# Output tiles of three pairs instead of four, in the same 48 KB, for the last 204 pairs of a pairwise bilinear kernel

## The chip, the cores and the metric

The kernel runs on one core of one Trainium2 chip. The metric is the device time of one execution in microseconds (us). A core has TensorE (PE: matmuls; PEld: its weight loads), VectorE (DVE), ScalarE (ACT), GpSimd (POOL), SyncE (SP), and 16 DMA engines that carry everything between the chip's memories. SyncE, ScalarE and GpSimd issue the DMAs, each on a queue of its own.

## The reference

There are 32 fields; each has, for 1024 rows of a batch, a vector of 128 numbers. For each of the 496 pairs of fields i < j there is a 128 x 128 matrix W. The result of a pair is the vector of field i times the pair's matrix, and that times the vector of field j, number by number:

```python
v_i = inputs[:, I_IDX, :]
v_j = inputs[:, J_IDX, :]
transformed = jnp.einsum('bpd,ped->bpe', v_i, W)
return transformed * v_j
```

All is in 32-bit floats. The output has 496 x 128 x 1024 of them, 260 MB; the inputs together have 49 MB.

## The kernel before, in words

**Tiles.** Fields lie on the chip as tiles of 128 partitions (the 128 numbers) by 1024 (the batch). The pairs are taken in the order of falling i and rising j; `q` is a pair's place in that order, 0 to 495. A pair's result is 128 x 1024, 4 KB a partition, 512 KB in all. It is made in two halves of 512, and `u = 2q + h` counts halves.

**One half.** The first 15 pairs are multiplied as plain 32-bit floats (L233). For all others the operands are split: ScalarE makes a high part (`wh` L142, `xh` L160), GpSimd the rest (`wl`, `wd` L144 to L146, `xl` L161 and L162), VectorE `xd` (L300). A half is then two matmuls (L236), a scaling of the sum in place by ScalarE (L238) and a third matmul that adds to it (L247), three halves later (`LAG`). There are four PSUM tiles `po`, so PE may be four pairs ahead of VectorE at most. VectorE multiplies a whole pair by field j and writes it to an output tile (L257, `ot`); the last two pairs go by halves (L255).

**Stores.** `OG = 4` pairs in succession share an output tile of 16 KB a partition (`out_tile`, L214). When the fourth is written, ScalarE issues one DMA for the tile (L284), 2 MB in rows of 16 KB. The issue stands in ScalarE's queue behind the scaling of the half that is five later (`SLAG` and `LAG`), and waits there for VectorE. The first group, and the last four pairs, are stored by single pairs or halves.

**Which tiles.** Three output tiles, s0 to s2, are there all the time (48 KB a partition). Four more, g0 to g3, are the places in which four fields each are loaded later on; until 20 pairs before that load (`until`, L211) they serve as output tiles too. `out_tile` takes the one that was used longest ago. From some pair on only s0, s1, s2 and g0 go round, and g0 is given up at pair 293, so that group 73 (pairs 292 to 295) is the first with three tiles alone. A tile is written again when its store has landed.

**Loads.** Matrices come eight pairs at a time (`load_w`, 512 KB), through SyncE, or as 448 KB through GpSimd and 64 KB through SyncE (`load_apart`, L106); a load is issued when the buffer before it has been split up. The fields of g0 are loaded from pair 313 on (`load_group`, L112), one in six pairs. `move_on` (L102) issues tiny loads through GpSimd.

**Order.** The order is written out by hand: the loop at L266 emits for each `u` the first part of that half, the second part of the half three before, stores that are due (L283), splits that are due (L285), loads and `xd`. Each engine takes its instructions in that order and waits on semaphores.

Of the kernel before, what the change touches and what calls it, by code (L numbers as in the profile page):

```python
# [7 lines left out]
F32 = mybir.dt.float32  # L8
F32R = mybir.dt.float32r
ALU = mybir.AluOpType  # L10

P = 128
NF = 32
NQ = NF * (NF - 1) // 2
BT = 1024
HB = 512
WC = 2
WL = 8
OG = 4
# [15 lines left out]
ROWS = 8 * NE  # L35
WAPART = tuple(range(12, 62, 2))
BACK = 3
XAT = (313, 219, 141, 52)
OWAIT = 20
XSTEP = 6  # L40
SLAG = 2
# [3 lines left out]
def _pairs():  # L45

    return [(i, j) for i in range(NF - 2, -1, -1) for j in range(i + 1, NF)]


@with_exitstack  # L50
def kernel(
# [21 lines left out]

    nc = tc.nc
    pairs = _pairs()
    nchunk = NQ // WC

    xpool = ctx.enter_context(tc.tile_pool(name="x", bufs=1))
# [3 lines left out]
    opool = ctx.enter_context(tc.tile_pool(name="o", bufs=1))  # L82
    ppool = ctx.enter_context(tc.tile_pool(name="ps", bufs=1, space=bass.MemoryType.PSUM))

    x_sb = {}
# [41 lines left out]
    scaled, taken, halved = {}, {}, {}  # L127

    def apart(inst, other, reason="the halves of a pair lie in two banks"):

        if other is not None:
            tc.declare_no_dep(inst.ins, other.ins, reason=reason)
# [75 lines left out]
    ngroup = NF // XG // 2  # L208
    group_at = {q + XSTEP * (XG - 1 - m): (k, m) for k, q in enumerate(XAT) for m in range(XG)}
    assert all(q + 5 < first_q[XG * k + m + 2] for q, (k, m) in group_at.items())  # L210
    until = {f"g{k}": q - OWAIT for k, q in enumerate(XAT)}  # L211
    used = {t: n - 9 for n, t in enumerate(("s0", "s1", "s2", *sorted(until, reverse=True)))}

    def out_tile(g):  # L214
        t = min((t for t in used if (g + 1) * OG <= until.get(t, NQ + OG)), key=used.get)
        used[t] = g
        pool = xpool if t in until else opool
        return pool.tile([P, OG, BT], F32, tag=t, name=f"ot_{g}")

    ctx.enter_context(tc.manual_schedule())  # L220
    po, ots, stores = {}, {}, []
# [19 lines left out]
    def second(u):  # L241
        q, h = divmod(u, 2)
        i, j = pairs[q]
        r = slice(q % WC * P, (q % WC + 1) * P)
        s = slice(h * HB, (h + 1) * HB)
        if q >= nq0:
            m = nc.tensor.matmul(  # L247
                po[q][:, s], w_s[q // WC][2][:, r], x_s[i][2][:, s], start=False, stop=True, skip_group_check=True
            )
            apart(m, scaled[u ^ 1])  # L250
        g, k = divmod(q, OG)
        if k == 0 and h == 0:
            ots[g] = out_tile(g)
        if q >= NQ - 2:
            nc.vector.tensor_tensor(ots[g][:, k, s], po[q][:, s], x_sb[j][:, s], ALU.mult)  # L255
        elif h == 1:
            taken[q] = nc.vector.tensor_tensor(ots[g][:, k, :], po.pop(q), x_sb[j], ALU.mult)  # L257
        if q >= NQ - 2:
            stores.append((u + SLAG, out[g, :, k, s], ots[g][:, k, s]))
        elif g == 0 or q >= NQ - OG:  # L260
            if h == 1:
                stores.append((u + SLAG, out[g, :, k], ots[g][:, k]))
        elif k == OG - 1 and h == 1:
            stores.append((u + SLAG, out[g], ots[g]))

    for u in range(2 * NQ + LAG + SLAG):  # L266
        q = u // 2
        if u < 2 * NQ:
            i, j = pairs[q]
# [11 lines left out]
        if LAG <= u < 2 * NQ + LAG:  # L281
            second(u - LAG)
# [7 lines left out]
        if ring[WB:] and ring[0] in spent:  # L290
# [6 lines left out]
            if c in WAPART:  # L297
                back.append(q + BACK)
        while later and later[0][0] <= u:
# [32 lines left out]
```

## Time and profile before

| | |
|---|---|
| median of 5 runs | 747.72 us (745.5 to 749.06) |
| the profiled execution: its own time | 748.25 us |
| its span, from first to last instruction | 746.5 us |
| busy: PE, DVE, ACT, POOL | 706.3, 637.9, 635.2, 596.6 us |
| moved by DMA | 310.02 MB, 415 GB/s over the span |
| output stores of 2048 KB | 122, 12.1 us from issue to landing in the median |

Busy time is the time in which an engine worked; one that waits is not busy. A DMA share near 1 over a stretch means that all 16 DMA engines had packets in work in it; the sum can come out at 1.01, since one packet's record can overlap the next by a little. A granted clock (PEclk) of 1.00 is TensorE at full speed. A line number, such as L257, is that of the listing above.

### The profile page before, as it was taken

Reading aid. Unit: us, or ns where it says so; the run is one execution under the profiler, and the core shown is the slowest. Engines: PE = TensorE matmul, PEld = TensorE weight load, DVE = VectorE, ACT = ScalarE, POOL = GpSimd, SP = SyncE. Lnnn points to the kernel's source line nnn. Section 1 sums busy time; section 2 is a strip of 40 time slices with the busy share of each in tenths; the row PEclk is TensorE's granted clock in tenths of the full one; section 3 lists DMA queues with packets and bytes.
Section 4 is the critical chain, followed back from the end, with each engine's and each line's share of the span. In section 5 each row is a group of like instructions: output and inputs, shape, how many; then the busy total and the mean of one; then the engine's idle time right before and its main releaser. Section 6 shows DMA issues by size and latency. Waiting matters only on the chain.

```text
span 746.5 us, 10290 instructions
## 1 busy us (share of the span) xinstructions
PE 706.3 (95%) x2946; PEld 550.1 (74%) x2946; DVE 637.9 (85%) x550; ACT 635.2 (85%) x1256; POOL 596.6 (80%) x882
## 2 busy tenths in 40 slices
PE   7999999999999999899899979998999999999994
PEld 3477777777778887677688858877877878777783
DVE  3898999999999998898799868878998989888885
ACT  1198989999999999798899968988988989888893
POOL 1789999999999999878779867977787888796660
PEclk9999999999999999999999989999999999999998
DMA  9999999999999999999999998999999999999998
GB/s 347 425 428 424 418 406 430 423 417 430 419 415 421 427 423 422 427 428 419 424 428 422 428 426 343 424 423 423 425 424 419 420 421 419 418 405 398 423 405 343
DMA packets 34664, 310.02 MB, mean 415 GB/s; under 512 B 5296, under 2 KB 5424, under 8 KB 18992
## 3 DMA queue, kind: packets, MB, share of 16 engines
q10 hardware_dynamic: 19584, 261.10, 83.1%
q1 hardware_dynamic: 10592, 36.77, 12.4%
q0 software_dynamic: 4432, 11.48, 4.1%
q8 instruction: 24, 0.39, 0.2%
q14 instruction: 32, 0.26, 0.1%
HBM read 49.29 MB, written 260.05 MB: 414 GB/s over the span
## 4 chain that ended last, share of the span: by engine, by line
PE 60%; DMA 23%; DVE 9%; POOL 3%; issue 2%; ACT 1%; DVEq 0%; ACTq 0%; POOLq 0%
PE po L236 38%; DMA out_dram<-ot 22%; PE po L247 19%; DVE ot L257 6%; PE po L233 4%; DVE xd L300 2%; POOL wd L146 1%; POOL wl L144 1%; POOL xl L161 1%; DMA x<-in_xt_dram 1%; ACT po L238 1%; POOL xl L162 0%; POOL wd L145 0%; DVE ot L255 0%; ACT wh L142 0%
## 5 line engine op out<-in xcount | busy, mean ns | idle before, releaser
L238 ACT ACTIVATE po<-po 128x512 f32<-128x512 f32 x962 | 553.3, 584 | 78.1 <-PE po L236 62.5
L257 DVE TENSOR_TENSOR ot<-po,x 128x1024 f32<-128x1024 f32 x358 | 430.5, 1221 | 74.6 <-DMA out_dram<-ot 25.4
L236 PE MATMUL po<-xh,wh 128*128 128x512 f32 x962 | 382.3, 397 | 22.2 <-DVE ot L257 21.4
L247 PE MATMUL po<-xd,wd 128*128 128x512 f32 x962 | 376.0, 391 | 4.8 <-DVE xd L300 2.4
L236 PE MATMUL po<-xl,wl 128*128 128x512 f32 x962 | 376.9, 392 | 1.3 <-POOL wl L144 0.9
L236 PEld LDWEIGHTS po<-xh,wh 128*128 128x128 f32 x962 | 181.0, 188 | 80.8 <-DVE ot L257 43.9
L144 POOL TENSOR_TENSOR wl<-w,wh 128x256 fp32r<-128x256 f32 x241 | 185.5, 770 | 68.5 <-ACT wh L142 62.3
L247 PEld LDWEIGHTS po<-xd,wd 128*128 128x128 f32 x962 | 181.0, 188 | 45.0 <-DVE ot L255 3.2
L236 PEld LDWEIGHTS po<-xl,wl 128*128 128x128 f32 x962 | 181.2, 188 | 41.0 <-POOL wl L144 4.0
L146 POOL TENSOR_TENSOR wd<-wl,wd 128x256 fp32r<-128x256 f32 x241 | 181.4, 753 | 20.1
L257 DVE TENSOR_TENSOR ot<-po,x_g 128x1024 f32<-128x1024 f32 x136 | 163.9, 1223 | 25.5 <-DMA out_dram<-ot 12.9
L145 POOL TENSOR_SCALAR wd<-wh 128x256 fp32r<-128x256 f32 x241 | 103.2, 428 | 20.5
L142 ACT ACTIVATE wh<-w 128x256 fp32r<-128x256 f32 x241 | 98.6, 410 | 8.3 <-DVE ot L257 5.8
L300 DVE TENSOR_TENSOR xd<-xh,xl 128x512 fp32r<-128x512 f32 x52 | 49.1, 944 | 0.0
L161 POOL TENSOR_TENSOR xl<-x_g,xh 128x512 fp32r<-128x512 f32 x32 | 41.7, 1302 | 3.2 <-ACT xh L160 3.0
L161 POOL TENSOR_TENSOR xl<-x,xh 128x512 fp32r<-128x512 f32 x20 | 25.8, 1292 | 15.8 <-ACT xh L160 15.5
L162 POOL TENSOR_SCALAR xl<-xl 128x512 fp32r<-128x512 f32 x52 | 34.4, 662 | 4.6
L233 PE MATMUL po<-x,w 128*128 128x512 f32 x60 | 30.5, 669 | 4.0 <-DMA x<-in_xt_dram 4.0
L233 PEld LDWEIGHTS po<-x,w 128*128 128x128 f32 x60 | 12.4, 212 | 21.3 <-issue 15.5
L160 ACT ACTIVATE xh<-x 128x512 fp32r<-128x512 f32 x20 | 12.3, 623 | 11.5 <-DMA x<-in_xt_dram 11.3
L160 ACT ACTIVATE xh<-x_g 128x512 fp32r<-128x512 f32 x32 | 20.0, 624 | 0.0
L104 POOL DMA_DIRECT2D mark<-in_xt_dram x26 | 16.6, 638 | 0.0
(7 smaller groups left out, 20.0 us busy)
## 6 DMA issues: line engine op xcount, KB each, us to landing
out_dram<-ot ACTq DMA_DIRECT2D x122, 2048.0 KB, 12.1
w<-in_wt_dram SPq DMA_DIRECT2D x36, 512.0 KB, 10.9
w<-in_wt_dram POOLq DMA_DIRECT2D x25, 448.0 KB, 11.9
x_g<-in_xt_dram SPq DMA_DIRECT2D x16, 512.0 KB, 16.5
x<-in_xt_dram SPq DMA_DIRECT2D x14, 512.0 KB, 9.6
out_dram<-ot ACTq DMA_DIRECT2D x6, 512.0 KB, 8.3
w<-in_wt_dram SPq DMA_DIRECT2D x26, 64.0 KB, 6.3
x<-in_xt_dram ACTq DMA_DIRECT2D x4, 256.0 KB, 5.9
```

Of the source, the lines that this page charges most:

```text
L142: halved[c] = nc.scalar.mul(h, raw, 1.0 - 2.0**-13)
L144: nc.gpsimd.tensor_tensor(l, raw, h.bitcast(F32), ALU.subtract)
L145: nc.gpsimd.tensor_scalar(d, h.bitcast(F32), EPS, 1.0, ALU.mult, ALU.mult)
L146: nc.gpsimd.tensor_tensor(d, l.bitcast(F32), d.bitcast(F32), ALU.subtract)
L161: nc.gpsimd.tensor_tensor(l, x_sb[f][:, s], h.bitcast(F32), ALU.subtract)
L162: nc.gpsimd.tensor_scalar(l, l.bitcast(F32), 1.0 / EPS, 1.0, ALU.mult, ALU.mult)
L233: nc.tensor.matmul(po[q][:, s], w_raw[q // WL][:, q % WL, :], x_sb[i][:, s], start=True, stop=True)
L236: m = nc.tensor.matmul(po[q][:, s], w_s[c][t][:, r], x_s[i][t][:, s], start=t == 0, stop=t == 1)
L238: scaled[u] = nc.scalar.mul(po[q][:, s], po[q][:, s], 1.0 + EPS)
L247: m = nc.tensor.matmul(po[q][:, s], w_s[q // WC][2][:, r], x_s[i][2][:, s], start=False, stop=True, skip_group_check=True)
L257: taken[q] = nc.vector.tensor_tensor(ots[g][:, k, :], po.pop(q), x_sb[j], ALU.mult)
L300: nc.vector.tensor_tensor(*later.pop(0)[1:], ALU.subtract)
```

## The change

The first 73 groups (pairs 0 to 291) stay as they are, four pairs each. From pair 292 on there are 68 groups of three pairs. The three tiles s0 to s2 become one tile `slots` of 12 places of one pair each (the same 48 KB a partition); a group of four on s0, s1 or s2 takes places 0 to 3, 4 to 7 or 8 to 11, and groups of three take places 0 to 2, 3 to 5, 6 to 8 and 9 to 11 in turn. Which store a product has to wait for is then found by places. `written` and `apart` declare that two products of VectorE on the same place need no wait on each other. The output in memory becomes one run of 496 pairs, in which a group of n pairs lies as 128 rows of n x 4 KB; the host puts it in order. The last group, pairs 493 to 495, is stored by a single pair and by halves, as the last four pairs were.

```diff
+FOURS = 73
+NS = 12
...
+def _groups():
+
+    return [(q, OG) for q in range(0, OG * FOURS, OG)] + [(q, OG - 1) for q in range(OG * FOURS, NQ, OG - 1)]
...
+    groups = _groups()
+    group_of = {q + k: (g, k) for g, (q, n) in enumerate(groups) for k in range(n)}
...
+    slots = opool.tile([P, NS, BT], F32, tag="slots", name="slots")
+    written = {}
+
     def out_tile(g):
-        t = min((t for t in used if (g + 1) * OG <= until.get(t, NQ + OG)), key=used.get)
-        used[t] = g
-        pool = xpool if t in until else opool
-        return pool.tile([P, OG, BT], F32, tag=t, name=f"ot_{g}")
+        q, n = groups[g]
+        if n < OG:
+            a = (g - FOURS) * n % NS
+        else:
+            t = min((t for t in used if q + n <= until.get(t, NQ)), key=used.get)
+            used[t] = g
+            if t in until:
+                return xpool.tile([P, OG, BT], F32, tag=t, name=f"ot_{g}"), None
+            a = OG * int(t[1:])
+        return slots[:, a : a + n, :], a
+
+    def rows(g):
+        q, n = groups[g]
+        return out[q : q + n].rearrange("q a -> (q a)").rearrange("(p k m) -> p k m", p=P, k=n)
+
+    def write(g, k, s, p, f):
+        ot, a = ots[g]
+        i = nc.vector.tensor_tensor(ot[:, k, s], p, f, ALU.mult)
+        if a is not None:
+            for h in (0, 1):
+                if s.start < (h + 1) * HB and s.stop > h * HB:
+                    apart(i, written.get((a + k, h)), "one engine writes both, in order")
+                    written[a + k, h] = i
+        return i
...
-        g, k = divmod(q, OG)
+        g, k = group_of[q]
...
-        elif g == 0 or q >= NQ - OG:
+        elif g in (0, len(groups) - 1):
             if h == 1:
-                stores.append((u + SLAG, out[g, :, k], ots[g][:, k]))
-        elif k == OG - 1 and h == 1:
-            stores.append((u + SLAG, out[g], ots[g]))
+                stores.append((u + SLAG, rows(g)[:, k], ot[:, k]))
+        elif k == n - 1 and h == 1:
+            stores.append((u + SLAG, rows(g), ot))
```

More of the change, by code (lines that the diff above doesn't have):

```diff
@@ L254, in second @@
         if q >= NQ - 2:
-            nc.vector.tensor_tensor(ots[g][:, k, s], po[q][:, s], x_sb[j][:, s], ALU.mult)
+            write(g, k, s, po[q][:, s], x_sb[j][:, s])
         elif h == 1:
-            taken[q] = nc.vector.tensor_tensor(ots[g][:, k, :], po.pop(q), x_sb[j], ALU.mult)
+            taken[q] = write(g, k, slice(0, BT), po.pop(q), x_sb[j])
+        ot = ots[g][0]
+        n = groups[g][1]
         if q >= NQ - 2:
-            stores.append((u + SLAG, out[g, :, k, s], ots[g][:, k, s]))
-        elif g == 0 or q >= NQ - OG:
+            stores.append((u + SLAG, rows(g)[:, k, s], ot[:, k, s]))
+        elif g in (0, len(groups) - 1):
             if h == 1:
-                stores.append((u + SLAG, out[g, :, k], ots[g][:, k]))
-        elif k == OG - 1 and h == 1:
-            stores.append((u + SLAG, out[g], ots[g]))
+                stores.append((u + SLAG, rows(g)[:, k], ot[:, k]))
+        elif k == n - 1 and h == 1:
+            stores.append((u + SLAG, rows(g), ot))
     for u in range(2 * NQ + LAG + SLAG):
@@ L323 @@
         args.append(nc.dram_tensor(f"in_{name}_dram", a.shape, mybir.dt.from_np(a.dtype), kind="ExternalInput").ap())
-    args.append(nc.dram_tensor("out_0_dram", (-(-NQ // OG), P, OG, BT), F32, kind="ExternalOutput").ap())
+    args.append(nc.dram_tensor("out_0_dram", (NQ, P * BT), F32, kind="ExternalOutput").ap())
     with tile.TileContext(nc) as tc:
@@ L329 @@
     y = _np.empty((BT, NQ, P), _np.float32)
-    y[:, perm, :] = got.transpose(3, 0, 2, 1).reshape(BT, -1, P)[:, :NQ]
+    for q, n in _groups():
+        y[:, perm[q : q + n], :] = got[q : q + n].reshape(P, n, BT).transpose(2, 1, 0)
     return y
```

## The prediction

> **What bounds the kernel now.** I read the page's slices and its DMA queues first, then the chain, then busy time by stretches, then VectorE in order of time around pair 292. From the page:
>
> ```profile
> DMA  9999999999999999999999998999999999999998
> GB/s 347 425 428 424 418 406 430 423 417 430 419 415 421 427 423 422 427 428 419 424 428 422 428 426 343 424 423 423 425 424 419 420 421 419 418 405 398 423 405 343
> ...
> q10 hardware_dynamic: 19584, 261.10, 83.1%
> ...
> PE 60%; DMA 23%; DVE 9%; POOL 3%; issue 2%; ACT 1%; DVEq 0%; ACTq 0%; POOLq 0%
> ```
>
> The 16 DMA engines are busy in nearly every slice; one slice (the 25th, 448 to 466 us) moves 343 GB/s instead of some 424. q10, the output stores, is 83% of their time. The chain names PE for 60%, but a chain walks through whatever was last at each step; PE's pace and the DMA's are close. One pair of halves is six matmuls; VectorE's undisturbed products stand 1.36 us apart (716.57, 717.93, 719.29 us), so PE alone would bring out 512 KB in 1.36 us, and the DMA at 424 GB/s takes 1.24 us for that plus the loads. So I ask by stretch who is full:
>
> ```profile
> core 0: us, PE busy (x) PEld busy (x) DVE busy (x) ACT busy (x) POOL busy (x), PEclk, DMA share, GB/s
> 20.00:430.00 410.00, 398.04 (x1677) 311.34 (x1676) 369.21 (x321) 362.60 (x722) 358.89 (x520) 1.00 1.01 423
> ...
> 438.00:444.00 6.00, 1.35 (x6) 0.77 (x5) 0.35 (x1) 2.00 (x5) 4.43 (x8) 0.88 1.02 433
> 444.00:448.00 4.00, 3.07 (x7) 2.51 (x8) 3.83 (x4) 1.05 (x2) 0.00 (x0) 0.50 0.99 426
> 448.00:449.50 1.50, 1.50 (x5) 1.14 (x4) 0.33 (x1) 0.69 (x2) 0.00 (x0) 0.54 0.59 251
> 449.50:451.25 1.75, 1.75 (x10) 1.40 (x9) 1.42 (x2) 1.39 (x3) 0.40 (x1) 1.00 0.13 56
> 451.25:453.25 2.00, 2.00 (x10) 1.67 (x9) 1.84 (x2) 1.79 (x5) 1.83 (x4) 1.00 0.94 393
> ...
> 470.00:700.00 230.00, 222.05 (x951) 176.28 (x951) 198.01 (x170) 206.22 (x407) 185.28 (x280) 1.00 1.01 419
> ...
> 716.00:735.00 19.00, 18.89 (x84) 15.31 (x82) 17.11 (x15) 17.03 (x33) 9.52 (x16) 1.00 0.94 395
> ...
> 744.00:745.00 1.00, 0.00 (x0) 0.00 (x0) 0.00 (x0) 0.00 (x0) 0.00 (x0) 0.50 0.12 47
> ```
>
> The column before the last is the DMA share. It is 1.01 from 20 to 430 us and from 470 to 700 us: **the DMA engines are full, and VectorE's waits for tiles cost nothing there**. They are idle in two places only. One hole lies at 448 to 451.5 us: 1.5 x 0.41 + 1.75 x 0.87 + 2 x 0.06 = 2.3 us in the mean over 16 engines. The other is the end, 716 to 735 us: 19 x 0.07 (against 1.01) = 1.3 us. But 0.13 is two engines of 16: two were busy all through the hole, and two (0.12) finish last, from 744 to 745. What makes the first hole:
>
> ```profile
> 432.19 5.02 DVE L257 TENSOR_TENSOR ot<-po,x 128x1024 f32<-128x1024 f32 x4 [0.27 <-DMA out_dram<-ot]
> 443.65 2.36 DVE L257 TENSOR_TENSOR ot<-po,x 128x1024 f32<-128x1024 f32 x2 [6.44 <-DMA out_dram<-ot]
> 445.92 0.68 DVE L300 TENSOR_TENSOR xd<-xh,xl 128x512 fp32r<-128x512 f32 x1
> 446.62 1.23 DVE L257 TENSOR_TENSOR ot<-po,x 128x1024 f32<-128x1024 f32 x1
> ```
>
> 443.65 is pair 292. Group 73 is the first that can't have g0 and goes to s0, whose store (group 70) lands at 443.53: 6.44 us of waiting. PE stands still, comes back at clock 0.50, and the next store is issued only at 450.56, when the four products are done.
>
> **The change part by part.**
>
> *The wait at pair 292 stays.* Slots 0 to 2 held pairs 280 to 282 of the same group 70, and one store carries them: in the order of the changed program pair 292 waits for the same semaphore as before. Pairs 296 and 300 also wait for the stores of groups 71 and 72 as before. Nothing is saved up to 447.9 us.
>
> *The first store comes earlier.* After three products (292, 293, 294; the last ends at 446.62 + 1.23 = 447.85) instead of four (450.41). ScalarE issues it after the scaling three pairs on, whose rows stand at 448.75 and 449.86, so at 449.3 instead of 450.56: the hole shrinks by 1.2 us, for the 14 engines that had run dry. For the two that never did, by nothing.
>
> *Packets.* Stores of 292 to 495 go out in rows of 12 KB. The trace's packet records have the median of a packet by size: 84 ns (2 KB), 140 (3.5 KB), 159 (4 KB), 611 (16 KB), 9 for the store's semaphore. From 4 to 16 KB that is 150.7 ns for 4 KB and 8 fixed, and the 3.5 KB row lies on the line, so a size that is no power of two costs nothing of its own; 12 KB: 460.3. An engine carries 8 rows of a store: four pairs 8 x 611 + 9 = 4897, 1224 ns a pair; three pairs 8 x 460.3 + 9 = 3691, 1230.5 a pair. 6.3 ns x 201 pairs (the last three go out singly) = **1.3 us more** on every engine. The late engines pay more: of the stores' packets the slowest twentieth takes 94 ns at 2 KB, 174 at 4 KB, 647 at 16 KB (the last in 715 to 735 us, without loads). That line has 16 ns fixed, and 136 packets more on an engine (67 stores of three, 536 rows, against 50 of four, 400) are 2.2 us. Ends 1.3 and 2.2; I take 1.7.
>
> *Sixteen stores more on ScalarE's queue*, 0.34 us each (row of the issue at 450.56). The next scaling starts 0.11 us after such an issue (450.67), beside it: 16 x 0.1 = 2 us of an engine that idles 20.8 us from 475 on. Nothing, while the DMA is full; if that cover went, 2 us. In the changed order a store also waits for the DMA eight issues earlier on SP's and ScalarE's queues, as before; eight issues are now some 17 pairs (24 us) against landings of 8.9 to 17.2 us, so it has landed. SP's loads have such waits too, and weights behind them; the same margin covers them.
>
> The Trainium skill ("DMA: Bandwidth & Descriptors", "Anatomy of one DMA") gives a DMA 2.0 us and its bytes at 436 GB/s, and its rule of sizes asks for 1 MiB and more a DMA, which 1.5 MB still is. If each store paid the 2.0 alone, 16 more would be an estimated 32 us by that page. Share 1.01 with two stores outstanding says that it lies beside the next store; the sum goes without it.
>
> *A longer lead.* At a boundary three tiles of three (9 pairs) may be outstanding instead of two of four (8), in the same 48 KB. With the engines full this only moves the waits. At the end it counts: PE's last wait for a tile ends at 706.1 us and from there products come at PE's pace to 739.2; one pair of lead is 1.2 us, and smaller stores leave shorter gaps. But at least three engines are busy at every instant of 716 to 735 us, by the packet records. Engines that idle there gain at most 1.3 us; those that end last gain nothing that the trace shows.
>
> *The sum* goes by the engines that end last: +1.7, less what they win from the hole. If the two of 450 us are the two of 745, that is 0; if others, at most their lag of 1.0 us behind the rest. The trace does not name engines: I take -0.4. +1.3 on the profiled execution's 748.25 us is 749.5. It lies 0.5 above the median of the five runs (747.72), so against the median: **749.0 us**.
>
> **Rivals.**
>
> *Holes filled (faster).* If the late engines change places, the hole (1.2, at most 2.3) and the end (1.3) are won, and 1.3 paid: -1.2 to -2.3, 745.4 to 746.5. For it: both idle places are caused by stores of four pairs. Against it: two engines are never idle.
>
> *Packets dearer (slower, the other side of no change).* One mechanism: in every store from pair 292 a 12 KB row costs an engine more than the line says. An engine has 536 such packets, so 1 ns is 0.54 us; the sum passes 0.3% (2.2 us, with -0.4 for the hole) when the rows cost 2.6 us, that is from (2.6 - 1.3) / 0.54 above 460, some 463 ns. If a row were moved as three of 4 KB (3 x 159 = 477), an engine would pay (8 x 477 + 9) / 3 - 1224 = 51 ns a pair, 10.3 us: 758. At the late engines' 16 ns of fixed cost alone it is 2.2 us, 749.9. For it: packets of those engines. Against 477: the 3.5 KB row, and 16 KB packets are recorded whole.
>
> *No lead at all.* A store lands when the last engine is done, and the late two lag by 3 to 4 us at pair 292, by the landings of the 16 engines; the fourth tile would then only wait on them, and the change is the packets alone: 1.3 to 2.2, 749.0 to 749.9. This lies beside the forecast.
>
> **How the numbers follow.** Measurement of this kernel tells some 0.3% (2.2 us) from no change: 745.5 to 750.0. Forecast and "no lead", within 0.3%: 0.55. Packets dearer: 0.30, most of it just beyond 750.0, a sixth of it near 758. Holes filled: 0.15, of which 0.10 below 745.5 and 0.05 within. So faster 0.10, same 0.60, slower 0.30. The range takes in the holes' case down to 745.6 and dearer packets up to some 468 ns (8 x 0.54 = 4.3 us more than the line says: 747.7 + 1.3 + 4.3 - 0.4 = 752.9); it leaves out the 758 and the case of all holes filled.
>
> **What would show it.** Right: pair 292 still waits about 6 us and PE drops to half clock; the first store after it comes at about 449.3; DMA share still 1.01 from 470 to 700; 67 stores of 1536 KB; 12 KB packets of 460 ns in the median; less idle in the last 30 us, and yet no earlier end. Wrong: a packet median over 465, a share below 1.0 between 470 and 700 (new waits), or an end with all 16 engines done together and earlier.

## The result, and the profile after

The changed kernel takes 747.53 us in the median of 45 runs, the kernel before 747.6 in 87 runs beside them; the ratio is 0.9987, 95% interval 0.9973 to 1.0002. That is -1.0 us, between -2.0 and +0.1 (the means, 746.61 and 747.57, differ by that; the medians by 0.1): no change that this measurement can tell, as forecast, and inside the range. But the sum of the prediction, +1.3 us, lies outside this interval: its terms need looking at.

The profiled execution of the changed kernel took 745.46 us (span 743.7). From its page, the slices and the stores:

```profile
DMA  9999999999999999999999999999999999999997
GB/s 345 427 422 430 427 414 427 426 422 428 424 421 425 425 423 424 426 423 425 422 429 424 423 426 398 424 419 429 420 417 418 417 422 418 419 418 404 415 419 309
...
out_dram<-slots ACTq DMA_DIRECT2D x67, 1536.0 KB, 12.6
out_dram<-slots ACTq DMA_DIRECT2D x44, 2048.0 KB, 16.3
```

The 25th slice now moves 398 GB/s instead of 343, and the last one 309 instead of 343: a gap has been closed in the middle and another has opened at the end. VectorE around pair 292:

```profile
431.63 2.58 DVE L244 TENSOR_TENSOR slots<-po,x 128x1024 f32<-128x1024 f32 x2
440.27 2.36 DVE L244 TENSOR_TENSOR slots<-po,x 128x1024 f32<-128x1024 f32 x2 [6.05 <-DMA out_dram<-slots]
442.54 0.68 DVE L334 TENSOR_TENSOR xd<-xh,xl 128x512 fp32r<-128x512 f32 x1
443.23 1.22 DVE L244 TENSOR_TENSOR slots<-po,x 128x1024 f32<-128x1024 f32 x1
```

The same view of ScalarE (its queue of DMA issues is ACTq), two rows of the kernel before and two of the changed one, with the first store behind pair 292:

```profile
448.75 0.58 ACT L238 ACTIVATE po<-po 128x512 f32<-128x512 f32 x1 [0.64 <-PE po L236]
450.56 0.34 ACTq L284 DMA_DIRECT2D out_dram<-ot  x1
...
445.36 0.58 ACT L270 ACTIVATE po<-po 128x512 f32<-128x512 f32 x1 [0.64 <-PE po L268]
445.43 0.34 ACTq L318 DMA_DIRECT2D out_dram<-slots  x1
```

Pair 292 (440.27) still waits 6 us for the same store. The first store behind it goes out 5.2 us after pair 292 starts (445.43), where before it was 6.9 us (443.65 to 450.56). By stretches (the column before the last is the DMA share):

```profile
core 0: us, PE busy (x) PEld busy (x) DVE busy (x) ACT busy (x) POOL busy (x), PEclk, DMA share, GB/s
...
440.00:444.00 4.00, 2.45 (x6) 1.97 (x7) 3.72 (x4) 0.58 (x1) 0.00 (x0) 0.52 1.01 433
444.00:448.00 4.00, 4.00 (x13) 3.15 (x12) 1.89 (x3) 2.46 (x5) 0.32 (x1) 0.63 0.99 422
448.00:450.00 2.00, 2.00 (x10) 1.64 (x10) 1.84 (x2) 1.62 (x4) 1.83 (x4) 1.00 1.00 426
450.00:452.00 2.00, 2.00 (x11) 1.65 (x10) 1.73 (x3) 1.97 (x5) 1.46 (x4) 1.00 0.99 324
...
480.00:700.00 220.00, 211.72 (x910) 168.90 (x909) 189.29 (x162) 196.82 (x390) 175.84 (x268) 1.00 1.01 418
...
735.00:739.00 4.00, 0.00 (x0) 0.00 (x0) 0.41 (x1) 0.00 (x0) 0.00 (x0) 0.50 0.95 372
739.00:742.50 3.50, 0.00 (x0) 0.00 (x0) 0.00 (x0) 0.00 (x0) 0.00 (x0) 0.50 0.22 86
```

In this execution the hole is gone (no stretch below 0.99 where 0.59 and 0.13 stood). From 480 to 700 the engines are as full as before. But in the last 3.5 us only 0.22 of the engines work: by the landings of the last store 11 of the 16 have finished at 739.1 us or before, and the last lands at 742.6. Counted from the packet records (us of idle time, mean over 16 engines):

| kernel | hole (420 to 480) | 700 us to the last product | last product to the end |
|---|---|---|---|
| before | 2.2 | 1.4 | 1.3 |
| changed | 0.2 | 0.7 | 3.0 |

2.7 us of idle time have been taken away where they were seen, and 1.7 have come back at the end. Single executions of these kernels differ by several us (741.5 to 751.3 in the 45 runs, and one of 754.1), so the two profiles alone settle nothing. Up to pair 292 both kernels do the same work in the same order, and there the two executions already differ by 3.4 us: pair 292 starts at 443.65 and at 440.27. From its start to the end of the span it is 302.8 us before and 303.4 after.

The last column comes back in the traces of the runs below (their numbers are those of the next section): 1.3 to 2.1 us in the five kernels in fours (before, 1, 2, 8 and 9), 2.7 to 4.5 in the eight that end in threes with 12 places. The hole does not. With threes it is 0.1 us in run 4 and 2.8 in run 12, which is the same kernel; with fours it is 0.8 in run 9 and 6.6 in run 8. It goes with how far the 16 engines are apart when pair 292 waits: the store that it waits for lands on the last engine 3.5 us after the first in the changed kernel, 6.4 in the kernel before, 4.0 in run 4, 8.6 in run 12, 3.9 in run 9, some 10.5 in runs 7, 8 and 10. So how much of the 2.0 us here is the change's, these two traces do not tell; at equal distance (8 and 7) threes take away 1.8 us.

### The profile page after: what moved, and what is told of

Its sections match the earlier page's. It is cut to its first block, busy times and chain, and to the rows that moved or that the text cites. A ratio compares the mean times of both kernels' runs of the same rounds, so it can differ in the third digit from the quotient of the medians.

```text
span 743.7 us, 10346 instructions
## 1 busy us (share of the span) xinstructions
PE 704.4 (95%) x2946; PEld 550.3 (74%) x2946; DVE 636.6 (86%) x550; ACT 634.2 (85%) x1256; POOL 596.8 (80%) x882
## 4 chain that ended last, share of the span: by engine, by line
PE 56%; DMA 26%; DVE 8%; POOL 3%; ACT 3%; issue 2%; ACTq 0%; SPq 0%; DVEq 0%; POOLq 0%
PE po L268 35%; DMA out_dram<-slots 19%; PE po L279 17%; DMA out_dram<-ot 7%; DVE slots L244 5%; PE po L265 3%; ACT po L270 3%; DVE xd L334 2%; DVE ot L244 1%; POOL wd L153 1%; POOL wl L151 1%; DMA x<-in_xt_dram 1%; POOL xl L168 1%; ACT wh L149 0%; POOL xl L169 0%
## 5 line engine op out<-in xcount | busy, mean ns | idle before, releaser
L244 DVE TENSOR_TENSOR slots<-po,x 128x1024 f32<-128x1024 f32 (+1 forms) x263 | 314.0, 1213 | 56.3 <-DMA out_dram<-slots 20.0
L244 DVE TENSOR_TENSOR slots<-po,x_g 128x1024 f32<-128x1024 f32 x123 | 148.1, 1223 | 26.3 <-DMA out_dram<-slots 13.3
L244 DVE TENSOR_TENSOR ot<-po,x 128x1024 f32<-128x1024 f32 x99 | 119.4, 1221 | 14.2 <-DMA out_dram<-ot 3.6
L334 DVE TENSOR_TENSOR xd<-xh,xl 128x512 fp32r<-128x512 f32 x52 | 47.6, 916 | 0.0
```

The lines of the kernel that those rows point to most:

```text
L244: i = nc.vector.tensor_tensor(ot[:, k, s], p, f, ALU.mult)
L334: nc.vector.tensor_tensor(*later.pop(0)[1:], ALU.subtract)
```

## The experiments

Two theories. **The engine that ends last sets the time**: a store has landed, and the kernel has ended, when the slowest of 16 DMA engines is done; time that the others idle is not on the path, so a filled hole only moves their idle time to the end, and the packets of 12 KB cost what they cost. **Idle places of all engines count**: each us of mean idle time that is filled is won. Where a ratio is given it is to the kernel before, run beside it on the same chip; runs 1 to 4, 5 to 8 and 9 to 12 each ran together.

**1. Packets alone.** All stores stay single DMAs of four pairs, with memory laid out pair by pair, so that rows are 4 KB.

```diff
-            stores.append((u + SLAG, out[g], ots[g]))
+            stores.append((u + SLAG, out[g].rearrange("k p m -> p k m"), ots[g]))
...
-    args.append(nc.dram_tensor("out_0_dram", (-(-NQ // OG), P, OG, BT), F32, kind="ExternalOutput").ap())
+    args.append(nc.dram_tensor("out_0_dram", (-(-NQ // OG), OG, P, BT), F32, kind="ExternalOutput").ap())
```

> The kernel before with every store still one DMA of four pairs, but laid out in memory pair by pair, so that its rows are 4 KB instead of 16 KB: packets alone, with no change in tiles, stores or waits. Price by the line of the packet records (159 ns for 4 KB, 611 for 16 KB): (32 x 159 + 9) / 4 = 1274 ns a pair against 1224, 50 ns x 492 pairs = 24.6 us, ratio to the kernel before 1.033. If the slowest engines pay by packet (16 ns fixed): 98 ns a pair, 48 us, ratio 1.06. If packets are hidden, so that the change's packets cost nothing: 1.000.

Measured: 772.04 us, ratio 1.0322 (1.0283 to 1.0361), +24.1 us. The interval is some 21 to 27 us. The line through the packet records is right within it (+24.6; the 122 stores are 488 pairs, not 492, which makes 24.4), so packets are on the path at about their price; the dearer packets of slow engines (+48) are out. From its page, the share of the DMA engines' time that stores take:

```profile
DMA packets 81512, 310.02 MB, mean 402 GB/s; under 512 B 5296, under 2 KB 5424, under 8 KB 81456
...
q10 hardware_dynamic: 66432, 261.10, 84.9%
```

The same 261.10 MB in 66432 packets instead of 19584, at 402 GB/s instead of 415.

**2. The form alone.** The changed kernel with groups of four to the end.

```diff
-    return [(q, OG) for q in range(0, OG * FOURS, OG)] + [(q, OG - 1) for q in range(OG * FOURS, NQ, OG - 1)]
+    return [(q, OG) for q in range(0, NQ, OG)]
...
-        if n < OG:
-            a = (g - FOURS) * n % NS
+        if q >= OG * FOURS:
+            a = (q - OG * FOURS) % NS
...
```

> The changed kernel with four pairs a group to the end: the form by places alone, tiles and packets as before. Theory 'the engine that ends last sets the time' and rival 'idle places of all engines count': both 1.000 against the kernel before, the hole at pair 292 of some 2.3 us still there. If the form itself changes a wait, another ratio, and the trace shows where.

Measured: 748.06 us, ratio 0.9994 (0.9964 to 1.0023); idle in the hole 2.4 us. The form costs and wins nothing that can be seen (the interval is some 2 to 3 us either way).

**3. Threes only where the engines ran dry.**

```diff
+    threes = lambda q: 292 <= q < 304 or q >= 460
...
+        out.append((q, 3 if threes(q) else 4))
...
```

> Threes only where the DMA engines ran dry: pairs 292 to 303 and 460 to 495, fours between. The extra packets fall to a quarter (0.4 us by the line). Theory 'the engine that ends last sets the time': the holes are filled for engines that don't end last, ratio 1.000 to 1.001. Rival 'idle places of all engines count': the hole (1.2 to 2.3 us) and the end (1.3 us) are won and 0.4 paid, -2.1 to -3.2 us, ratio 0.996 to 0.997.

Measured: 747.73 us, ratio 1.0008 (0.9975 to 1.0041). The hole is mostly filled (0.6 us of idle time), yet from the last product to the end it has 3.1 us, against 1.3 in the kernel before. The rival's 0.996 to 0.997 is just outside the interval; the first theory's 1.000 to 1.001 is inside.

**4. No loads through GpSimd from the 36th on.**

```diff
-WAPART = tuple(range(12, 62, 2))
+WAPART = tuple(range(12, 36, 2))
```

> The changed kernel with the matrices from the 36th load on all issued plainly through SyncE: 13 loads that gave two engines one packet each and the other 14 nine give all 16 eight. The bytes stay the same. Theory 'the engine that ends last sets the time': the two engines get 13 x 7 x 159 ns = 14.5 us more; they end up to 3 us before the last now, so +11 to +14.5 us against the changed kernel, ratio to before 1.013 to 1.018. Rival 'the mean over the engines counts': 0 us, or up to 2.7 less since GpSimd's loads disturb no packets any more, ratio 0.995 to 1.000.

Measured: 745.44 us, ratio 0.9970 (0.9940 to 1.0001). A miss for the first theory as I had put it: the two engines that GpSimd's loads were taken to spare are not the ones that end last, or are slow only while GpSimd loads. The theory that the last engine counts does not need them to be.

**5. No tiny loads (`move_on`) from pair 270 on**, so that, by the expectation, the spared pair goes round.

```diff
-            if u % 2 == 0 and q in back:
+            if u % 2 == 0 and q in back and q < 270:
```

> The changed kernel without the tiny loads of move_on from pair 270 on. These bring GpSimd's loads of 14 engines back to the same start, so that two engines are always spared; without them the spared pair goes round, and from the second of the last 12 loads on the two engines that were spared carry 8 packets of 159 ns in most of them: some 10 x 8 x 159 ns = 12.7 us more on these two, as much less on the others together. Bytes and the mean over the engines stay the same. Theory 'the engine that ends last sets the time', with the spared engines slow of themselves while GpSimd loads: +8 to +12 us against the changed kernel, ratio to before 1.010 to 1.015. Rival 'the mean counts': 0, ratio 0.997 to 1.001.

Measured: 747.86 us, ratio 1.0001 (0.9974 to 1.0029). The second miss on the same point, by the same reasoning: if the spared pair goes round, it makes no difference above 0.3% which engines are spared in the second half, and "the late engines are the spared ones" falls. That the pair does go round is not shown, since the trace does not number the engines.

**6. Three tiles of three.** Less lead, the same packets.

```diff
-            a = (g - FOURS) * n % NS
+            a = (g - FOURS) * n % NT
```

with `NT = 9`.

> The changed kernel with three tiles of three pairs from pair 292 (36 KB, 9 places) instead of four: packets and number of stores as in the change, lead 6 pairs outstanding at a boundary instead of 9. Theory 'the engine that ends last sets the time': 14 engines run dry often, the late ones hardly ever, since 6 pairs are 7.4 us of DMA against some 6 us from a landing to the next store: 0 to +3 us against the change, ratio to before 0.999 to 1.003. Rival 'idle places of all engines count' (each hole is paid): up to 1 us at each of 67 stores, ratio 1.02 to 1.09. If the fourth tile's lead is what the change wins, well above the change.

Measured: 750.69 us, ratio 1.0041 (1.0013 to 1.0069): by the ratios some 4 us above the changed kernel (2 to 6), a little over the first theory's 0 to 3 and far below the rival's 1.02. Its stretches:

```profile
430.00:470.00 40.00, 33.04 (x136) 25.88 (x135) 27.85 (x25) 29.48 (x59) 26.91 (x42) 0.96 0.94 376
470.00:700.00 230.00, 221.37 (x947) 175.29 (x945) 196.90 (x171) 204.59 (x405) 183.85 (x280) 1.00 1.01 415
700.00:743.00 43.00, 40.00 (x172) 31.70 (x170) 37.01 (x33) 35.60 (x69) 22.59 (x36) 1.00 0.97 407
```

From 470 to 700 us two outstanding stores of three keep the engines full (1.01) as well as three do. What the fourth tile is worth, and where, this trace does not show: behind pair 292 the hole is 2.8 us, but so it is in run 12 with four tiles and the engines as far apart (9.0 and 8.6 us). Pair 292 starts 5.0 us later than in the changed kernel, before the fourth tile can matter, and from there to the end it is 303.8 us against 303.4.

**7 and 8. The change where runs lie close together.** All loads through SyncE, in the changed kernel (7) and in the kernel before (8).

```diff
-WAPART = tuple(range(12, 62, 2))
+WAPART = ()
...
-            if u == 2 * nq0:
-                move_on(5)
```

> The changed kernel with every load through SyncE, none through GpSimd. The packets that lasted longer than the usual 611 and 159 ns stood around GpSimd's loads: 207 us summed over 16 engines in the kernel before, 13 us an engine at most to be won. Against it, two engines are no longer spared: 25 x 7 x 159 ns = 28 us more on each if they are slow of themselves. Theory 'slow through GpSimd's loads only': ratio to before 0.985 to 0.997, runs closer together. Rival 'slow of themselves': 1.02 to 1.04.

> The kernel before with every load through SyncE: partner of the changed kernel with plain loads, to see the change alone where runs lie closer together. 'The engine that ends last sets the time': the changed kernel is 1.3 us (its packets) slower than this one. 'Idle places of all engines count': the changed kernel wins the hole and the end (2.5 to 3.6 us) and pays 1.3: 1.2 to 2.3 us faster than this one. In both the hole after pair 292 is there in this kernel and nearly gone in the changed one.

Measured: threes 754.18 us (753.66 to 754.45, ratio 1.0078, 1.0048 to 1.0107), fours 753.14 (752.80 to 753.71, ratio 1.0065, 1.0045 to 1.0085). Both of number 7's own ideas missed: plain loads are slower than GpSimd's, but not by 2%. What helps is the spread: the ten runs of 8 and the six of 7 lie within 0.9 us each, where the 26 runs of the kernel before beside them went from 743.8 to 752.2. Here the change costs **+1.0 us**, near the first theory's +1.3; the rival's -1.2 to -2.3 is out. And the hole became smaller all the same (6.6 us of idle time to 4.8). The stretches of the fours (8):

```profile
449.00:450.00 1.00, 0.03 (x1) 0.04 (x1) 1.00 (x2) 0.00 (x0) 0.00 (x0) 0.50 0.54 229
450.00:456.75 6.75, 6.75 (x19) 5.34 (x20) 4.60 (x5) 3.21 (x6) 0.64 (x1) 0.60 0.08 34
...
747.00:749.00 2.00, 0.00 (x0) 0.00 (x0) 0.00 (x0) 0.00 (x0) 0.00 (x0) 0.50 0.62 234
749.00:750.50 1.50, 0.00 (x0) 0.00 (x0) 0.00 (x0) 0.00 (x0) 0.00 (x0) 0.50 0.05 19
```

The threes (7), in the same columns:

```profile
449.00:450.00 1.00, 0.44 (x1) 0.44 (x2) 1.00 (x2) 0.00 (x0) 0.00 (x0) 0.50 0.16 66
450.00:454.25 4.25, 4.25 (x13) 3.34 (x13) 3.10 (x4) 1.86 (x4) 0.00 (x0) 0.62 0.06 27
...
745.00:748.00 3.00, 0.00 (x0) 0.00 (x0) 0.00 (x0) 0.00 (x0) 0.00 (x0) 0.50 0.40 152
748.00:751.00 3.00, 0.00 (x0) 0.00 (x0) 0.00 (x0) 0.00 (x0) 0.00 (x0) 0.50 0.05 20
```

In fours the engines stand at 0.54 and 0.08 for 7.75 us, in threes at 0.16 and 0.06 for 5.25. A share of 0.06 is one engine: one alone works through the hole, and one alone works in the last us (whether it is the same, the trace does not say). The landings of stores on their 16 engines show how far the last is behind (us; the 14th, 15th and last engine to finish the store):

```
store of pairs 288 to 291, fours:  14th 450.92  15th 452.46  last 458.48
store of the next group, fours:    14th 463.59  15th 463.59  last 463.98
store of pairs 288 to 291, threes: 14th 450.31  15th 450.40  last 458.16
store of the next group, threes:   14th 458.91  15th 458.93  last 462.75
last store, fours:                 14th 748.57  15th 749.58  last 750.47
last store, threes:                14th 746.48  15th 747.35  last 750.85
```

At pair 292 one engine is 7.6 us behind the 14th. In fours the 15 others wait in the hole until it has caught up (0.4 us). In threes they wait less and it stays 3.8 us behind. At the end the 14th engine of the threes is 2.1 us earlier (746.48 against 748.57), and the last one is 0.4 us later: the gain is there, in 14 engines that don't set the end.

**9. Fours with the loads of 4**, the kernel before with the edit of 4.

> The kernel before with the matrices from the 36th load on through SyncE alone: partner, in fours, of the changed kernel with the same loads (run 4: 745.4 us, all its runs within 744.6 to 748.3). There the latest engine was only 0.4 to 1.3 us behind the 14th around pair 292, so in fours the latest engine must run dry too. Theory 'the engine that ends last sets the time': it idles about 2.3 - 1.0 = 1.3 us in the hole, as much as the packets cost (1.3): the change is worth -0.5 to +0.5 us here, this kernel at 745 to 746, ratio 0.996 to 0.998. Rival 'idle places of all engines count': 1.2 to 2.3 us slower than run 4.

**10. Mixed groups, all loads through SyncE**, the edits of 3 and 7 together.

> All loads through SyncE, threes only for pairs 292 to 303 and 460 to 495, fours between. Hole filled as far as with threes throughout (1.8 us of mean idle time less), a quarter of the extra packets (0.3 us). One engine is 7.6 to 9 us late at pair 292 and never dry in either of the two kernels of this kind. Theory 'the engine that ends last sets the time': 753.1 (fours) + 0.3 = 753.4 us, between 753.0 and 753.7. Rival 'idle places of all engines count': 753.1 - 1.8 + 0.3 = 751.6 us or less. If not the packets but the lead or the waits made threes 1.0 us slower: 753.8 to 754.2.

**11. Mixed groups with the loads of 4**, the edits of 3 and 4 together.

> The loads of run 4 with threes only for pairs 292 to 303 and 460 to 495. The hole filled and only a quarter of the packets' price. Theory 'the engine that ends last sets the time': 0.5 to 1.0 us less than run 4 where its latest engine is fed by the same threes, 744.4 to 745.0, ratio to before 0.995 to 0.997. Rival 'idle places of all engines count': the same 1.0 less; this run is to see whether a version beats both kernels beyond its interval.

**12. The kernel of 4 again**, beside 9 to 11.

> The kernel of run 4 once more, on the chip of the other three, so that fours, threes and the mixed form are compared on the same chip: 744.6 to 748.3 us, ratio 0.994 to 1.000 as before. Fours against this one: within 0.5 us by 'the engine that ends last', 1.2 to 2.3 slower by 'idle places of all engines count'.

Measured: 10 takes 753.23 us (752.91 to 753.95; ratio 1.0082, 1.0050 to 1.0115). In us that is the first theory's 753.4, not the rival's 751.6. Its hole (4.9 us) is as small as that of the threes, and its median is that of the fours:

```profile
449.00:450.00 1.00, 0.44 (x1) 0.44 (x2) 1.00 (x2) 0.00 (x0) 0.00 (x0) 0.50 0.24 98
450.00:454.25 4.25, 4.25 (x13) 3.30 (x13) 3.08 (x4) 1.84 (x4) 0.00 (x0) 0.62 0.07 31
```

This points to the threes between pairs 304 and 459, three quarters of the packets, as what makes the 1.0 us between 7 and 8, and not the hole or the groups just behind pair 292. It does not show it. Run 10 did not run together with 7 and 8, the kernel before was some 1 us faster beside it, and by the ratios (1.0082 with 0.3% either way) it may lie with the threes (1.0078) as well. For the reading by us speak the traces: pair 292 starts at 448.28 us in 7 and in 10 and at 448.69 in 8, and from there to the end of the span it is 303.6 us in 7, 302.8 in 10 and 302.8 in 8, each a single execution.

9 takes 745.5 us (ratio 0.9989, 0.9965 to 1.0012), 11 takes 746.02 (0.9995, 0.9969 to 1.0021), 12 takes 746.74 (1.0000, 0.9978 to 1.0023). The hole of 9 was 0.8 us, not the 2.3 that its expectation took, so there was less to win. Fours are not slower than threes here, which speaks against the rival's 1.2 to 2.3, but the intervals hold everything from -2 to +3 us. Number 12 is the same kernel as 4, which had 0.9970: what one such comparison shows below 0.3% can't be built on, and no version here beats both kernels beyond its interval.

## Why the prediction was right, point by point

*No change, as forecast, and why.* The forecast class and the range were right, with room to spare: all terms are small against the 0.3% that counts as no change, so a sum that was off by 2.3 us (+1.3 against -1.0) still came out right. That is margin and not precision. The mechanism is shown by 1, 7 and 8, in kernels that are not the changed one itself: the DMA engines are full, 4 KB packets are paid at about their price, and what is won in idle places is won by engines that don't end last. For the changed kernel, with GpSimd's loads, it is argued from these.

*The wait at pair 292 stays:* right (6.05 us, 6.44 before). *The first store comes 1.2 us earlier:* right in kind, small in size: counted from the start of pair 292 it came 1.7 us earlier (5.16 us behind it instead of 6.91), since it goes out 0.07 us after the start of the third scaling (445.36; 448.75 before) and not midway to the fourth. In 7 and 8 it was 2.2 us earlier (5.16 against 7.38). The hole went from 2.2 to 0.2 us in the profiled executions and from 6.6 to 4.8 from 8 to 7.

*Packets, 1.7 us:* the term between its two ends was taken too high. 12 KB packets have a median of 460 ns as worked out. Run 1 bears out the price by the line of medians (24.1 us measured, between 21 and 27, for 24.4), which makes 1.3 us of the change's packets, and 7 against 8 shows 1.0 for the whole change. The upper end, 2.2 from the slowest packets, is out: its counterpart in run 1 would have been 48 us. What the packets of the last engine took the trace does not tell apart; the means over all engines from pair 292 on, 625 ns for 16 KB in 8 and 467 for 12 KB in 7 (1252 and 1248 ns a pair with the semaphore's 9), do not show the price.

*Sixteen more stores on ScalarE's queue, and its waits for earlier DMAs, nothing:* no run takes them alone, but the DMA share of 1.01 from 480 to 700 us, and the 1.0 us of 7 against 8 in all, leave little room for a cost beside the packets'. Of the 32 us that the prediction estimated by the Trainium skill ("DMA: Bandwidth & Descriptors", "Anatomy of one DMA", where the 2.0 us are a fit to DMAs that GpSimd issues, and not ScalarE as here), nothing is seen.

*A longer lead that those engines which end last don't use:* right: the last product came 7.2 us before the last landing instead of 6.1, and the 11 first engines ended 3.5 us before the last. But the sign "less idle in the last 30 us" did not come: from 700 us to the end there are 3.7 us of idle time instead of 2.7, since the engines that are done early idle at the very end.

*The sum.* +1.3 us against a measured -1.0, between -2.0 and +0.1. Packets were mis-sized: 1.7 that should have been 1.0 to 1.3. With that the sum is +0.6 to +0.9 and still above the interval. The term left is the last one, "less what they win from the hole", 0 to 1.0, of which -0.4 was taken: if the interval holds, the latest engine won 0.5 to 2.9 us more than that in the kernel with GpSimd's loads. That is possible there: around pair 292 the latest engine was 3.2 to 4.1 us behind the 14th in the profiled execution of before, but only 0.5 to 1.2 in that of the changed kernel, and 7.6 and more without those loads; an engine that is hardly behind can run dry with the others. Up to pair 292 both kernels do the same, so how far the last engine is behind changes from execution to execution. That this makes up the difference is argued, not shown: runs 2, 3, 9, 11 and 12 have intervals of 0.2 to 0.3% either way, too wide to tell.

*The rivals.* "Holes filled" described half of what the profile shows (the hole gone, but not the end) and not the time. "Packets dearer" needed 463 ns and more; the median is 460, and run 1 leaves no dearer price. "No lead at all" put the cause in the late engines, as the runs without GpSimd's loads do; but the lead was there, and the time did not rise by its 1.3 to 2.2.

## What to carry to other kernels

Where a DMA's data goes over many DMA engines, look at the landing of each engine before counting a gap in the mean share as a gain: a gap that the last engine works through was worth nothing here (7 against 8). Price smaller rows from the packet records by size; such a line gave 24.4 us here where 24.1 were measured, between 21 and 27. Compare two profiles up to the point where the programs part before reading their difference: here 3.4 us of it lay ahead of the change. And where a change is smaller than the run-to-run spread, find a variant of the kernel whose runs lie close together and make the comparison there, remembering that it answers for that variant.

## What the runs showed of the hardware that was not expected

With every load through SyncE the runs of one kernel lay within 0.9 us (752.8 to 753.7, ten runs of 8); with loads of 448 KB through GpSimd the 26 runs of the kernel before beside them went from 743.8 to 752.2. The time is lower with them (ratio 1.0065 for the kernel without).

One DMA engine can fall far behind with equal work: 7.6 to 9.3 us behind the 14th at 420 to 451 us in runs 7 and 8, without a single load through GpSimd, against 3.2 to 4.1 with them in the kernel before and 0.5 to 1.2 in the changed one. The Trainium skill ("DMA: Bandwidth & Descriptors", "Latency and other measured facts") says that engines 7 and 15 are usually slower and names GpSimd's descriptor rings as its best guess at the cause, not a certain one. Here the lag was larger in the two runs without a load through GpSimd, so it has another cause there. The trace does not number the engines, so whether it is one of these two no run here shows. Nor do the runs tell whether the engine would be as late with those loads and equal work, since 14 of the 16 carry them (`NE`, L34).

TensorE's clock was granted at half for 6.8 us around the wait of 6 us at pair 292, in both kernels (442.5 to 449.4 us before, 440.2 to 447.0 after). That this costs no time is argued, not shown: at least two DMA engines worked on through the hole of before, and at least 12 in the changed kernel.
